# Block 0 of a latent-attention kernel: other staging places for weights, own tiles per position, latents in three loads, the rotary stack in two halves

## The chip, the core and the metric

The kernel runs on one core of one Trainium2 chip. The time is the device time of one execution in microseconds (us). Before the change three runs took 1594.83, 1597.79 and 1601.57 us; the median, 1597.79, is the figure to compare with. A further execution, recorded by the hardware profiler, took 1599.18 us; everything called "the profile" below comes from that one.

Engines go by these names: PE is TensorE (matrix products; "PEld" is its loading of stationary operands), DVE is VectorE, ACT is ScalarE, POOL is GpSimd, and SP is SyncE, which here only issues DMA. Each engine works through a queue of its own in order; ACT and POOL issue DMAs too. An instruction that has to wait holds up whatever stands behind it in its engine's queue.

## The reference

One layer with multi-head latent attention (16 heads, 2048 tokens, hidden size 512), then a linear layer, each with a residual and a layer norm:

```python
# x: [1, 2048, 512]; H=16, DN=128, DR=64, DV=128, query latent 384, key/value latent 128
cq = rms_norm(x @ w_qa.T, q_a_ln_w)                      # query latents [2048, 384]
q = (cq @ w_qb.T).reshape(b, s, H, DN + DR)              # per head: 128 plain + 64 rotary columns
q_pe = q_pe * cos + rotate_half(q_pe) * sin
ckv = x @ w_kva.T                                        # [2048, 128 + 64]
k_pe = rotary(ckv[..., 128:])                            # one rotary key for all heads
kv = rms_norm(ckv[..., :128], kv_a_ln_w) @ w_kvb.T       # per head: k_nope 128, v 128
scores = q_full @ k_full.T * (DN + DR) ** -0.5           # causal, float32 softmax
out = softmax(scores) @ v                                # [2048, 16 * 128]
x = layernorm(x + out @ w_o.T)
x = layernorm(x + x @ (weight * scale_weight[:, None]).T + bias)
```

## The kernel before

**Arithmetic.** Matrix products in single precision are made of three products of split operands: `split` (L61 to L68) writes the high part with ACT (L64, or L67 with a scale) and the rest with DVE (L65, L68). The projection of keys and values is never made per head. Instead the plain part of `w_qb` is multiplied with the key part of `w_kvb` (`weights_q`, L131 to L171), so that queries meet the 128-wide latent keys directly, and the values are the latents too. `Kn` and `Kp` (each 128 x 2 x 2048) hold all keys, the latent and the rotary part, transposed, in a high and a low plane.

**Tiling.** Queries go in four blocks of 512 rows (`b` = 0 to 3), heads in eight pairs (`p`), and a block in four positions (`qt`) of 128 rows. Block `b`, position `qt` sees `nk = (4b + qt + 1) * 128` keys. A score tile is called `s_b_p_qt` below, its values `o_b_p_qt`. `units` (L615 to L679) runs over pairs and positions. In block 0 one position of a pair is: scores of both heads in one PSUM tile (`pair_scores`, L496; its products L410), row maxima on DVE (L504), exponentials on ACT into `pr` (L510), then `pair_probs` (L518): the normalised probabilities in two half-precision parts `hl` (ACT L522, DVE L523), and one transposing DMA on SP (L524) from `hl` into `PT`. `values` (L529) multiplies `PT` with the latents in `V` (PE L540), ACT copies the result to `ot` (L545), and a DMA takes it to DRAM. `PT` is a stretch of a ring of three slots in SBUF, `ring0`, that `room` gives out; values run behind the scores by a lag in positions (L616: 2 in block 0, at most 3 later).

**Block 0 prepares everything else.** Only the first 512 rows are projected ahead. While block 0's attention runs, two side generators are advanced by the position loop (L658 to L662): `rest_of_x` makes keys, values and query latents for the other 1536 rows in half blocks `hb` = 2 to 7 (`project_x`, L187 to L265: `xr` loads on ACT's queue, keys, three tiles `ps_cq`, their squares `sq` and `acc` at L251 and L253), and `rest_of_w` makes the weights of head groups 2 and 3 (`weights_q`; group 1 is made before the loop). `query_norms` sums `acc` over partitions with PE (L272) for the norm of the query latents. Latents and weights go out to DRAM buffers `cq_d`, `wq_d`, `wpe_d` and come back when a block or a group needs them: `load_block` (L299), `load_wq` (L311), `load_wpe`. In block 0 these loads are issued by POOL, later by SP.

**Buffers.** Raw pieces of input (`xr`, and in `weights_q` `rpe` and `wqb`) share four buffers, tag `wraw`; ACT issues their loads. Split pieces on their way to DRAM (`wpst` L146, `wst` L161, `cqst` L245) share the tag `st` with two buffers of 128 x 2 x 512 words. `pr` and `hl` have two buffers each, from the pool `blk0` (L120), for all positions. PSUM in block 0 has four tiles "m" (projections, weights, values) and two score tiles "s".

**Rotary queries.** `project_pe` (L324 to L366) works on a group of four heads: two products per group, `prod` on DVE (L341), the two sums (L348, L349; POOL except for group 0), `ph` on ACT (L351), and the stack: for each head two copies (ACT in block 0 and for the first group of block 1, L360; POOL otherwise, L362) and two subtractions (DVE in those cases, except that for group 0 heads 1 and 3 are POOL's; POOL otherwise; L363) into `pe`. All four heads are one step. `project_nope` (L369 to L391) makes the plain queries `qn` of one pair and, after its second head, issues the next weight load; for the last pair of a block also the loads of the next block's latents, `cq`, 1.5 MB as one DMA, and of its cosines, `cs`.

**Order.** In block 0 the queues of all engines are laid out by a scheduler ahead of time (`schedule_with_timeline_sim=True`, L971): the written order gives priorities, and an instruction is taken when its operands and its buffers are free in the scheduler's model. So a buffer that comes free earlier can move an instruction forward in its queue. From block 1 on the order of PE and SP is the written one (`manual_schedule`, L783). `fillers` is a list of generators, `fill` (L551) advances the first one by a step; in block 0 it is called once after each position's scores and probabilities, and the projections of the next pair are what it holds.

Of the kernel before, what the change touches and what calls it, by code (L numbers as in the profile page):

```python
# [9 lines left out]
F16 = mybir.dt.float16  # L10
BF16 = mybir.dt.bfloat16
F32 = mybir.dt.float32
# [7 lines left out]
P = 128  # L20
# [3 lines left out]
LT = 3  # L24
# [25 lines left out]
def mla_block(ctx: ExitStack, tc: tile.TileContext, a, out):  # L50
# [7 lines left out]
    def move(queue, dst, src):  # L58
        queue.dma_start(dst.bitcast(F32), src.bitcast(F32))
# [57 lines left out]
    ctx_a = ctx.enter_context(ExitStack())  # L117
    psum["m"] = ctx_a.enter_context(tc.tile_pool(name="ps_m0", bufs=4, space=PSUM, side="right"))
    psum["s"] = ctx_a.enter_context(tc.tile_pool(name="ps_s0", bufs=2, space=PSUM))
    blk0 = ctx_a.enter_context(tc.tile_pool(name="blk0", bufs=2))  # L120
    pa = ctx_a.enter_context(tc.tile_pool(name="pa", bufs=1))
    pa2 = ctx_a.enter_context(tc.tile_pool(name="pa2", bufs=2))

    def split_tile(raw, n, name, step):
        h = pa.tile([P, KT, n], F32R, name=f"{name}_h")
        l = pa.tile([P, KT, n], F32R, name=f"{name}_l")
        for i in range(0, KT, step):
            split(raw[:, i : i + step], h[:, i : i + step], l[:, i : i + step])
        return h, l

    def weights_q(g, direct=None):  # L131

        if direct is None:
            wk = pa.tile([P, 4, P], F32, tag="wk", name=f"wk{g}")
            nc.scalar.dma_start(wk, a["wk"][:, 4 * g : 4 * g + 4])
        else:
            wk = direct[2]
        for lt in range(LT):
            sc = qln[:, lt : lt + 1]
            if direct is None:  # L140
                raw = pa2.tile([P, 256], F32, tag="wraw", name=f"rpe{g}_{lt}", bufs=4)
                nc.scalar.dma_start(raw, a["wpe"][:, lt, g])
            else:
                raw = direct[4][:, lt]
            if direct is None:
                to = pa2.tile([P, 2, 256], F32R, tag="st", name=f"wpst{g}_{lt}")  # L146
            else:
                to = direct[1][:, :, lt]
            split(raw, to[:, 0], to[:, 1], sc)
            move(nc.sync, wpe_d[g][:, :, lt], to)  # L150
        for lt in range(LT):
            sc = qln[:, lt : lt + 1]
            if direct is None:
                raw = pa2.tile([P, 4, P], F32, tag="wraw", name=f"wqb{g}_{lt}", bufs=4)
                nc.scalar.dma_start(raw, a["wqb"][g, :, lt])
            else:
                raw = direct[3][:, lt]
            ps = psum["m"].tile([P, 512], F32, tag="m", name=f"ps_wq{g}_{lt}")
            for j in range(4):
                nc.tensor.matmul(ps[:, j * P : (j + 1) * P], raw[:, j, :], wk[:, j, :], start=True, stop=True)  # L160
            st = pa2.tile([P, 2, 512], F32R, tag="st", name=f"wst{g}_{lt}")  # L161
            if direct is None:
                split(ps, st[:, 0], st[:, 1], sc)
                move(nc.sync, wq_d[g][:, :, lt], st)
            else:
                to = direct[0][:, :, lt]
                split(ps[:, :256], to[:, 0], to[:, 1], sc)
                split(ps[:, 256:], st[:, 0, 256:], st[:, 1, 256:], sc)
                move(nc.sync, wq_d[g][:, :, lt, :256], to)
                move(nc.sync, wq_d[g][:, :, lt, 256:], st[:, :, 256:])  # L170
            yield  # L171

    def value_output(p, pool, tag):
# [13 lines left out]
    def project_x(hb, wkv, wqa, direct=None, raws=None):  # L187
# [47 lines left out]
        for lt in range(LT):  # L235
            ps = psum["m"].tile([P, 512], F32, tag="m", name=f"ps_cq{hb}_{lt}")
            n = 0
            for kt in range(KT):
                for w_, x_ in ((wqa[0], xh), (wqa[0], xl), (wqa[1], xh)):
                    nc.tensor.matmul(  # L240
                        ps[:, :256], w_[:, kt, lt * P : (lt + 1) * P], x_[:, kt, :], start=n == 0, stop=n == 11
                    )
                    n += 1
            if direct is None:
                st = pa2.tile([P, 2, 256], F32R, tag="st", name=f"cqst{hb}_{lt}")  # L245
                split(ps[:, :256], st[:, 0], st[:, 1])
                move(nc.sync, cq_d[b][:, :, lt, half], st)
            else:
                split(ps[:, :256], direct[:, 0, lt, half], direct[:, 1, lt, half])
            sq = pa2.tile([P, 256], F32, tag="sq", bufs=1, name=f"sq{hb}_{lt}") if lt else acc  # L250
            nc.scalar.activation(sq, ps[:, :256], AF.Square, scale=(LT * P) ** -0.5)  # L251
            if lt:
                nc.vector.tensor_tensor(acc, acc, sq, ALU.add)  # L253
            if lt == 1:
                pt = psum["m"].tile([P, 2, 2, P], F32, tag="m", name=f"ps_kt{hb}")
                for i, (nk, kp) in enumerate(flip):
                    nc.tensor.transpose(pt[:, 0, i, :], nk, ident)
                    nc.tensor.transpose(pt[:, 1, i, :], kp.rearrange("p a d -> p (a d)"), ident)
                cols = slice(hb * 256, (hb + 1) * 256)
                for k_, K in ((0, Kn), (1, Kp)):  # L260
                    split(pt[:, k_].rearrange("p a c -> p (a c)"), K[:, 0, cols], K[:, 1, cols])
            yield
# [36 lines left out]
    def load_block(b):  # L299
        if b == NB:  # L300
            return
        cq = prj.tile([P, 2, LT, QB], F32R, tag="cq", name=f"cq{b}")
        if b:
            move(state["queue"], cq, cq_d[b])
        cs = prj.tile([P, 2, QB], F32, tag="cs", name=f"cs{b}")
        (state["queue"] if b else nc.sync).dma_start(cs, a["csq"][b])
        state["cq"], state["cs"] = cq, cs
# [16 lines left out]
    def project_pe(b, g, direct=None):  # L324
# [30 lines left out]
        for j in range(4):  # L355
            q = slice(32 * j, 32 * j + 32)
            for x in range(2):
                to = pe[32 * x : 32 * x + 32, j, :]
                if quick:
                    nc.scalar.activation(to, rp[q, x, :], AF.Copy)  # L360
                else:
                    nc.gpsimd.tensor_copy(to, rp[q, x, :])  # L362
                (nc.gpsimd if not quick or (b, g) == (0, 0) and j % 2 else nc.vector).tensor_tensor(  # L363
                    pe[64 + 32 * x : 96 + 32 * x, j, :], rp[q, x, :], ph[q, x, :].bitcast(F32), ALU.subtract
                )
        state["pe", b, g] = pe  # L366
        yield

    def project_nope(b, p, direct=None):  # L369
        if direct is None and ("wq", b, p) not in state:  # L370
            load_wq(b, p)
        w = state.pop(("wq", b, p)) if direct is None else direct
        cq = state["cq"]
        qn = blk.tile([P, 2, 2, QB], F32R, tag="qn", name=f"qn{b}_{p}")
        for j in range(2):
            ps = psum["m"].tile([P, QB], F32, tag="m", name=f"ps_qn{b}_{p}_{j}")
            n = 0
            for lt in range(LT):
                for i, k in ((0, 0), (0, 1), (1, 0)):
                    nc.tensor.matmul(  # L380
                        ps, w[:, i, lt, j * P : (j + 1) * P], cq[:, k, lt, :], start=n == 0, stop=n == 8
                    )
                    n += 1
            split(ps, qn[:, 0, j, :], qn[:, 1, j, :], kvln)
            if j == 1:
                state["qn", b, p] = qn
                if b or p == NPAIR - 1:
                    load_wq(*((b, p + 1) if p + 1 < NPAIR else (b + 1, 0)))
                if p == NPAIR - 1:
                    load_block(b + 1)  # L390
            yield  # L391

    def project(b, p):
# [102 lines left out]
    def pair_scores(pool, b, p, qt, nk):  # L496
# [7 lines left out]
        nc.vector.tensor_reduce(neg, ps[:, :, :nk], axis=AX.X, op=ALU.max, negate=True)  # L504
        bias = small.tile([P, 2], F32, tag="bias", name="bias")
        nc.vector.tensor_scalar(bias, neg, r, None, ALU.mult)
        pr = pool.tile([P, 2, nk], F32, tag="pr", name=f"pr{b}_{p}_{qt}")
        sums = small.tile([P, 2], F32, tag="sums", name="sums")
        for j in range(2):
            nc.scalar.activation(  # L510
# [5 lines left out]
        return pr, inv  # L516

    def pair_probs(pool, b, p, qt, nk, PT, pr, inv):  # L518
        hl = pool.tile([P, 2, 2, nk], F16, tag="hl", name=f"hl{b}_{p}_{qt}")
        for j in range(2):  # L520
            iv = inv[:, j : j + 1]
            nc.scalar.activation(hl[:, j, 0, :], pr[:, j, :], AF.Copy, scale=iv)  # L522
# [90 lines left out]
                pass  # L613

    def units(pool, ring, b):  # L615
        lag = min(ring.shape[1] // (2048 * (b + 1)) - 1, 3)  # L616

        for p in range(NPAIR):
            put_in(True)
# [23 lines left out]
            for qt in range(4):  # L643
# [2 lines left out]
                    ctx_f.enter_context(tc.manual_schedule(engines={ET.PE, ET.SP, ET.DVE, ET.Activation}))  # L646
                if (b, p, qt) == (0, NPAIR - 1, 3):
                    s0, PT = -4 * nk, prj.tile([P, 4 * nk], F16, tag="ph", name="carry")
                else:
                    s0 = room(2048 * (b + 1), ring.shape[1], 4 * nk, (b, p) == (2, NPAIR - 1) and qt > 0)  # L650
                    PT = ring[:, s0 : s0 + 4 * nk]
# [110 lines left out]
                    stop=p == NPAIR - 1 and j == 1 and n == 2,  # L762
                )

    ring0 = pa.tile([P, 3 * 2048], F16, name="ring0")
    units(blk0, ring0, 0)
    for g in side:
        for _ in g:
            pass
# [205 lines left out]
```

## Time and profile before

| | |
|---|---|
| three runs, median (lowest to highest) | 1597.79 us (1594.83 to 1601.57) |
| the profiled execution | 1599.18 us |
| its span, first to last instruction | 1597.4 us |
| mean granted TensorE clock | 0.992 |
| busy share: PE, DVE, ACT, POOL | 97%, 73%, 58%, 23% |
| 0 to 265 us (block 0 and preparation): PE, DVE, ACT busy; clock; DMA share | 239.0, 190.5, 177.2 us; 0.96; 0.76 |
| 265 to 1280 us: PE busy; clock; DMA share | 1008.0 of 1015 us; 1.00; 0.82 |
| 1280 to 1597 us: PE busy; clock; DMA share | 303.7 of 317 us; 0.99; 0.47 |
| DMA traffic | 262.5 MB in 633,032 packets, 570,288 of them under 512 bytes |

How the lines are read that follow. The first part of a page gives each engine's busy time and share of the span, and its number of instructions. The second cuts the span into 40 equal slices; a digit is the busy share of a slice in tenths. A line of windows gives a stretch's bounds and length, then busy time and instruction count of PE, PEld, DVE, ACT and POOL, the granted clock of TensorE as a fraction of full speed, the busy share of the 16 DMA engines, and GB/s. A line of waits names the waiting engine, operation and source line, behind the arrow what it waited for, and then total time, number of times and the longest. A line of one instruction has its start, its duration, engine, line and operation, output and inputs with shapes, and in brackets its wait before the start and the releaser. A line on DMAs gives the issuing queue, the tile, the duration of the issuing instruction, and under it the time from issue to landing.

### The profile page before, as it was taken

Reading aid. Unit: us, or ns where it says so; the run is one execution under the profiler, and the core shown is the slowest. Engines: PE = TensorE matmul, PEld = TensorE weight load, DVE = VectorE, ACT = ScalarE, POOL = GpSimd, SP = SyncE. Lnnn points to the kernel's source line nnn. Section 1 sums busy time; section 2 is a strip of 40 time slices with the busy share of each in tenths; the row PEclk is TensorE's granted clock in tenths of the full one; section 3 lists DMA queues with packets and bytes.
Section 4 is the critical chain, followed back from the end, with each engine's and each line's share of the span. In section 5 each row is a group of like instructions: output and inputs, shape, how many; then the busy total and the mean of one; then the engine's idle time right before and its main releaser. Section 6 shows DMA issues by size and latency. Waiting matters only on the chain. (4 is left out here: it accounts for less than half of the span.)

```text
span 1597.4 us, 24700 instructions
## 1 busy us (share of the span) xinstructions
PE 1550.6 (97%) x9130; PEld 1293.8 (81%) x9130; DVE 1164.0 (73%) x2099; ACT 926.1 (58%) x1631; POOL 364.6 (23%) x434
## 2 busy tenths in 40 slices
PE   8898998999999999999999999999999998999997
PEld 7777877888888788888888888888888886788886
DVE  6777777888787878787787777777777775455564
ACT  5767676666665766767765665665666665321120
POOL 2333234252206305050022400400400000022132
PEclk9999999999999999999999999999999999999999
DMA  6888667789897987888896888878678798433230
GB/s 210 255 211 223 173 187 163 163 165 184 166 208 159 180 158 165 164 160 168 154 222 137 165 146 168 157 144 168 137 144 170 155 230 190 145 112 129 92 113 33
DMA packets 633032, 262.49 MB, mean 164 GB/s; under 512 B 570288, under 2 KB 611376, under 8 KB 631888
## 3 DMA queue, kind: packets, MB, share of 16 engines
q1 hardware_dynamic: 621472, 233.62, 68.1%
q0 software_dynamic: 4672, 17.73, 3.6%
q10 hardware_dynamic: 6768, 9.57, 2.1%
q8 instruction: 72, 1.18, 0.3%
q14 instruction: 48, 0.39, 0.1%
HBM read 83.17 MB, written 35.13 MB: 74 GB/s over the span
## 5 line engine op out<-in xcount | busy, mean ns | idle before, releaser
L410 PE MATMUL s<-Kn,qn 128*128 128x512 f32 (+4 forms) x1920 | 519.5, 376 | 6.2 <-ACT pr L463 4.4
L463 ACT ACTIVATE pr<-s,bias,rq 128x1024 f32<-128x1024 f32 (+3 forms) x320 | 324.6, 1018 | 215.0 <-DVE bias L457 157.9
L540 PE MATMUL o<-ring,V 128*128 128x256 f16 x3252 | 395.5, 274 | 12.2 <-DMA ring<-hl 5.2
L487 DVE SCALAR_TENSOR_TENSOR hl<-pr,inv,hl 128x1024 f16<-128x1024 f32 (+7 forms) x320 | 359.4, 1136 | 40.0 <-ACT hl L484 35.2
L410 PEld LDWEIGHTS s<-Kn,qn 128*128 128x128 f32 x1920 | 338.6, 190 | 52.9 <-ACT pr L463 7.8
L540 PEld LDWEIGHTS <-V 128*128 128x128 f16 x3264 | 303.7, 98 | 92.5 <-issue 52.8
L410 PE MATMUL s<-Kp,pe 128*128 128x512 f32 (+4 forms) x1280 | 360.4, 362 | 0.0
L484 ACT ACTIVATE hl<-pr,inv 128x1024 f16<-128x1024 f32 (+7 forms) x320 | 294.5, 961 | 92.6 <-issue 34.4
L448 DVE TENSOR_REDUCE neg<-s 128x1 f32<-128x1024 f32 (+3 forms) x320 | 317.8, 993 | 37.3 <-PE s L410 34.2
L410 PEld LDWEIGHTS s<-Kp,pe 128*128 128x128 f32 x1280 | 233.1, 188 | 29.6
L348 POOL TENSOR_TENSOR prod<-prod 128x512 f32<-128x512 f32 x15 | 19.3, 1288 | 641.9 <-DVE prod L341 641.9
L380 PE MATMUL ps_qn<-cq,wq 128*128 128x512 f32 x576 | 147.0, 400 | 4.1 <-ACT ot L545 3.3
L757 PE MATMUL acc<-wvo,oh 128*128 128x512 f32 x448 | 144.2, 403 | 0.0
L363 POOL TENSOR_TENSOR pe<-prod,ph 32x512 fp32r<-32x512 f32 x92 | 140.4, 1526 | 11.0 <-issue 5.1
L380 PEld LDWEIGHTS ps_qn<-cq,wq 128*128 128x128 f32 x576 | 108.3, 192 | 25.9 <-ACT ot L545 3.9
L757 PEld LDWEIGHTS acc<-wvo,oh 128*128 128x128 f32 x448 | 83.6, 189 | 21.2 <-issue 3.8
L475 DVE TENSOR_SCALAR inv<-sums 128x1 f32<-128x1 f32 x128 | 27.0, 211 | 98.6 <-ACT pr L463 98.5
L757 PE MATMUL acc<-wvo,ol 128*128 128x512 f32 x224 | 88.2, 394 | 0.0
L336 PE MATMUL ps_pe<-cq,wpe 128*128 128x512 f32 x288 | 71.9, 395 | 1.5 <-DMA cq<-cq_d 1.4
L545 ACT ACTIVATE ot<-o 128x256 f32<-128x256 f32 x128 | 48.4, 379 | 40.9 <-PE o L540 37.1
L362 POOL CAST pe<-prod 32x512 fp32r<-32x512 f32 x88 | 66.8, 760 | 3.3
L64 ACT ACTIVATE oh<-o 128x1024 fp32r<-128x1024 f32 x28 | 29.7, 1061 | 65.1 <-PE acc L757 51.8
(140 smaller groups left out, 1586.1 us busy)
## 6 DMA issues: line engine op xcount, KB each, us to landing
wq<-wq_d SPq DMA_DIRECT2D x22, 768.0 KB, 5.7
o<-ot_d SPq DMA_DIRECT2D x32, 512.0 KB, 3.3
ot_d<-ot SPq DMA_DIRECT2D x97, 128.0 KB, 2.3
wpe<-wpe_d SPq DMA_DIRECT2D x10, 768.0 KB, 5.4
wq<-wq_d POOLq DMA_DIRECT2D x9, 768.0 KB, 6.4
wq_d<-wst SPq DMA_DIRECT2D x9, 512.0 KB, 4.4
cq_d<-cqst SPq DMA_DIRECT2D x18, 256.0 KB, 3.5
wo<-in_wo_dram SPq DMA_DIRECT2D x4, 1024.0 KB, 6.2
```

The lines of the kernel that those rows point to most:

```text
L336: nc.tensor.matmul(ps, w[:, i, lt, x * P : (x + 1) * P], cq[:, k, lt, :], start=n == 0, stop=n == 8)
L362: nc.gpsimd.tensor_copy(to, rp[q, x, :])
L363: (nc.gpsimd if not quick or (b, g) == (0, 0) and j % 2 else nc.vector).tensor_tensor(pe[64 + 32 * x : 96 + 32 * x, j, :], rp[q, x, :], ph ...
L380: nc.tensor.matmul(ps, w[:, i, lt, j * P : (j + 1) * P], cq[:, k, lt, :], start=n == 0, stop=n == 8)
L410: nc.tensor.matmul(ps[:, :w], lhs, K[:, i, c0 : c0 + w], start=n == 0, stop=n == 4)
L448: nc.vector.tensor_reduce(neg[:, ti : ti + 1], v, axis=AX.XY, op=ALU.max, negate=True)
L463: nc.scalar.activation(pr[:, c0 : c0 + n * w].rearrange("p (a c) -> p a c", a=n), v, AF.Exp, bias=bias, scale=r, accum_out=sums[:, ti : ti ...
L484: nc.scalar.activation(hl[:, 0, c], pr[:, c], AF.Copy, scale=inv)
L487: nc.vector.scalar_tensor_tensor(hl[:, 1, c], pr[:, c], inv, hl[:, 0, c], ALU.mult, ALU.subtract)
L540: nc.tensor.matmul(ps[:, :256], vt[:, i, k % 4, :], v[:, :, l, k, :], start=n == 0, stop=n == 3 * kts - 1)
L545: nc.scalar.activation(ot, ps[:, :256], AF.Copy)
L757: nc.tensor.matmul(acc, l[:, t, c], state["wvo"][p][:, i, j, :], start=p == 0 and j == 0 and n == 0, stop=p == NPAIR - 1 and j == 1 and n ...
```

## The change

All of it concerns block 0 and the preparation beside it, but for the order and number of the latents' loads, which also holds for the later blocks.

1. *Weights staged where late keys will lie.* `places` names the columns 1024 to 1535 and 1536 to 2047 of `Kn` and `Kp`, which are written with keys only by half blocks 4 to 7 of `rest_of_x`. The split pieces of `wq` of groups 1 to 3 (L161) and those of `wpe` of groups 2 and 3 (L146; two of three pieces, each in half of `A`) are put there before they go to DRAM. Only the pieces that are left use `st` tiles, which are now half as large and three.
2. *Own tiles for each position.* `pr`, `hl` and `PT` of block 0 have a tag for each of the four positions with one buffer each, in place of two buffers for all and the ring; the lag of the values in block 0 is written as 2, the value that it had.
3. *Query latents in three loads.* `load_block` issues one DMA for each third of `cq` (0.5 MB) in place of one, and stands ahead of `load_wq`.
4. *The rotary stack in two halves.* For block 0 and the first group of block 1, heads 0 and 1 are one step and heads 2 and 3 another, which is appended to `fillers`. The subtractions of group 0 that were POOL's are DVE's.

```diff
-    blk0 = ctx_a.enter_context(tc.tile_pool(name="blk0", bufs=2))
+    blk0 = ctx_a.enter_context(tc.tile_pool(name="blk0", bufs=1))
...
+    A, B, C, D = (K[:, :, c : c + 512] for c in (1536, 1024) for K in (Kn, Kp))
+    places = [
+        [(None, None, None), (B, C, D)],
+        [(A[:, :, :256], A[:, :, 256:], None), (B, C, A)],
+        [(A[:, :, :256], A[:, :, 256:], None), (B, A, B)],
+    ]
...
-            if direct is None:
-                to = pa2.tile([P, 2, 256], F32R, tag="st", name=f"wpst{g}_{lt}")
+            if direct is not None:
+                to = direct[1][:, :, lt]
+            elif places[g - 1][0][lt] is not None:
+                to = places[g - 1][0][lt]
             else:
-                to = direct[1][:, :, lt]
+                to = pa2.tile([P, 2, 256], F32R, tag="st", name=f"wpst{g}_{lt}", bufs=3)
...
-            st = pa2.tile([P, 2, 512], F32R, tag="st", name=f"wst{g}_{lt}")
             if direct is None:
+                st = places[g - 1][1][lt]
                 split(ps, st[:, 0], st[:, 1], sc)
...
-                st = pa2.tile([P, 2, 256], F32R, tag="st", name=f"cqst{hb}_{lt}")
+                st = pa2.tile([P, 2, 256], F32R, tag="st", name=f"cqst{hb}_{lt}", bufs=3)
...
-        if b:
-            move(state["queue"], cq, cq_d[b])
+        for lt in range(LT if b else 0):
+            move(state["queue"], cq[:, :, lt], cq_d[b][:, :, lt])
...
+        def stack(heads):
+            for j in heads:
...
+                    (nc.vector if quick else nc.gpsimd).tensor_tensor(
...
+            yield
+
         state["pe", b, g] = pe
-        yield
+        if quick:
+            fillers.append(stack((2, 3)))
+            yield from stack((0, 1))
+        else:
+            yield from stack(range(4))
...
+                if p == NPAIR - 1:
+                    load_block(b + 1)
                 if b or p == NPAIR - 1:
                     load_wq(*((b, p + 1) if p + 1 < NPAIR else (b + 1, 0)))
-                if p == NPAIR - 1:
-                    load_block(b + 1)
...
-        pr = pool.tile([P, 2, nk], F32, tag="pr", name=f"pr{b}_{p}_{qt}")
+        pr = pool.tile([P, 2, nk], F32, tag=f"pr{qt}", name=f"pr{b}_{p}_{qt}")
...
-        hl = pool.tile([P, 2, 2, nk], F16, tag="hl", name=f"hl{b}_{p}_{qt}")
+        hl = pool.tile([P, 2, 2, nk], F16, tag=f"hl{qt}", name=f"hl{b}_{p}_{qt}")
...
-        lag = min(ring.shape[1] // (2048 * (b + 1)) - 1, 3)
+        lag = min(ring.shape[1] // (2048 * (b + 1)) - 1, 3) if b else 2
...
+                elif b == 0:
+                    s0, PT = -4 * nk, pool.tile([P, 4 * nk], F16, tag=f"PT{qt}", name=f"PT{p}_{qt}")
...
-    ring0 = pa.tile([P, 3 * 2048], F16, name="ring0")
-    units(blk0, ring0, 0)
+    units(blk0, None, 0)
```

More of the change, by code (lines that the diff above doesn't have):

```diff
@@ L166, in weights_q @@
                 to = direct[0][:, :, lt]
+                st = pa2.tile([P, 2, 256], F32R, tag="st", name=f"wst{g}_{lt}", bufs=3)
                 split(ps[:, :256], to[:, 0], to[:, 1], sc)
-                split(ps[:, 256:], st[:, 0, 256:], st[:, 1, 256:], sc)
+                split(ps[:, 256:], st[:, 0], st[:, 1], sc)
                 move(nc.sync, wq_d[g][:, :, lt, :256], to)
-                move(nc.sync, wq_d[g][:, :, lt, 256:], st[:, :, 256:])
+                move(nc.sync, wq_d[g][:, :, lt, 256:], st)
             yield
@@ L354, in project_pe @@
         quick = b == 0 or (b, g) == (1, 0)
[L355 to L365, printed above, removed]
-        state["pe", b, g] = pe
-        yield
+        def stack(heads):
+            for j in heads:
+                q = slice(32 * j, 32 * j + 32)
+                for x in range(2):
+                    to = pe[32 * x : 32 * x + 32, j, :]
+                    if quick:
+                        nc.scalar.activation(to, rp[q, x, :], AF.Copy)
+                    else:
+                        nc.gpsimd.tensor_copy(to, rp[q, x, :])
+                    (nc.vector if quick else nc.gpsimd).tensor_tensor(
+                        pe[64 + 32 * x : 96 + 32 * x, j, :], rp[q, x, :], ph[q, x, :].bitcast(F32), ALU.subtract
+                    )
+            yield
+        state["pe", b, g] = pe
+        if quick:
+            fillers.append(stack((2, 3)))
+            yield from stack((0, 1))
+        else:
+            yield from stack(range(4))
     def project_nope(b, p, direct=None):
```

## The prediction

> **What bounds the kernel now.** I read the page first, then the stretches of the first 265 us, then the waits of TensorE (PE) and ScalarE (ACT) there. The page:
>
> ```profile
> span 1597.4 us, 24700 instructions
> PE 1550.6 (97%) x9130; PEld 1293.8 (81%) x9130; DVE 1164.0 (73%) x2099; ACT 926.1 (58%) x1631; POOL 364.6 (23%) x434
> ...
> PE   8898998999999999999999999999999998999997
> ```
>
> A slice is 40 us. From slice eight on TensorE is nearly always busy; only the first seven, block 0 and what is prepared beside it, have holes. The change lies there, so its worth is time in which TensorE stood still before about 263 us. Four stretches of that time (columns: window, length, busy us and instruction count of PE, PEld, DVE, ACT, POOL, granted TensorE clock, DMA share, GB/s):
>
> ```profile
> 40.00:60.00 20.00, 16.39 (x98) 14.07 (x97) 16.13 (x28) 15.18 (x33) 7.56 (x7) 0.91 0.86 271
> ...
> 80.00:100.00 20.00, 16.14 (x95) 13.43 (x94) 15.33 (x32) 15.32 (x35) 10.88 (x17) 0.91 0.87 188
> ...
> 130.00:150.00 20.00, 15.13 (x93) 12.14 (x92) 15.69 (x36) 12.91 (x36) 6.22 (x9) 1.00 0.98 255
> 150.00:160.00 10.00, 8.78 (x41) 7.26 (x42) 7.48 (x14) 9.30 (x20) 4.15 (x8) 0.66 0.69 176
> ```
>
> VectorE (DVE) and ACT have slack on average, and the DMA engines are nearly full. A hole costs twice: by itself, and by the clock. 0.91 over 20 us is 1.8 us lost, 0.66 over 10 us is 3.4 us. Who held TensorE between 20 and 265 us (total, times, longest):
>
> ```profile
> PE ps_rq L272 <- DVE acc L253: 4.3, 1, 4.3
> PE o L540 <- ACT ot L545: 3.8, 1, 3.8
> PE ps_wq L160 <- DMA wqb<-in_wqb_dram: 3.4, 2, 2.4
> PE ps_qn L380 <- ACT ot L545: 1.9, 1, 1.9
> PE s L410 <- ACT pr L510: 1.8, 2, 1.6
> ```
>
> With the smaller rows this is 20.9 us. Add the clock, 1.8 three times (40 to 60, 80 to 100, 245 to 265) and 3.4 once: **29.7 us is all that block 0 can give**. Behind ACT stand buffers:
>
> ```profile
> ACT hl L522 <- DMA ring<-hl: 11.5, 4, 5.2
> ACT wst L67 <- DMA wq_d<-wst: 8.9, 3, 4.3
> ...
> ACT wst L67 <- DMA cq_d<-cqst: 5.2, 2, 3.3
> ```
>
> ACT wants to write a tile whose last contents are still being stored or transposed, and everything in its queue waits along.
>
> **The change, part by part.**
>
> *Staging in the late keys, three half-size `st` tiles.* No arithmetic is added or taken away. ACT loses its 16.0 us of waits at `wst` (8.9 + 5.2 + 1.9, the last for a `wpe_d` store). The new places are reused late; one new wait can bite: the split of `wpe` of group 3 goes into `Kn` just after the store of `wq` of group 2 left there, four ACT steps earlier. A store landed after 3.7 to 7.6 us in the 135 to 152 us stretch, the TensorE work between is about 4 us: 0 to 3.6 us on ACT, 1 taken, covered by ACT's slack. The 4.3 us hole is this part's best case. ACT's queue there:
>
> ```profile
> 149.36 0.69 ACT L67 ACTIVATE wst<-ps_wq,qln 128x512 fp32r<-128x512 f32 x1 [2.71 <-DMA wq_d<-wst]
> ...
> 149.95 0.38 ACT L251 ACTIVATE sq<-ps_cq 128x256 f32<-128x256 f32 x1
> ```
>
> The square `sq`, which `acc` and then the norm's matmul wait for, stood behind the held `wst`. In the changed order of ACT it also moves up, ahead of pair 3's exponentials. The stretch from 141 to 158 us cost 1.6 (a PSUM tile not yet read by DVE) + 4.3 + clock 3.4 = 9.3 us. Bounds 0 and 9.3; I take 8.5.
>
> *Own tiles for each position.* The 11.5 us at `hl` go: each position's tile was last read a whole pair earlier. The longest is at 242.78 us, where ACT stood 5.23 us. PT per position drops the SP queue's waits for ring space; their readers are two positions behind, at no cost or gain.
>
> *The rotary stack in two halves.* For group 0, POOL's four subtractions go to DVE. In the trace the shared case is visible: DVE's four take 0.683 to 1.69 us each, together 5.74 us, while POOL's four run at 1.6 us. Eight alone on DVE are 8 x 0.683 = 5.5 us: even; but heads 0 and 1 are ready after four, 2.7 us. POOL issues the `wpe` load of group 1 some 3 us earlier, no longer behind its subtractions. In the changed queues the later stacks are emitted nearly unbroken all the same: 0.
>
> *Latents in three loads, ahead of `wq`.* On POOL two more issues at 0.56 us, 1.1 us, ahead of `wq` and the `ot` stores; nobody on the path waits for those stores. For blocks 2 and 3 two more issues on SP at 0.6 us each time, 2.4 us in all, ahead of transposes whose readers come 8 us later; uncovered they would cost those 2.4 us, and I take 0. `wq` comes 1.5 MB later, and is needed some 20 us after its issue. For block 1 TensorE waited 1.4 us for the latents (one load of 9.7 us from issue to landing).
>
> *The order that follows.* Block 0's queues are made by the scheduler, and freed tiles let it pull work forward. Two pulls matter.
>
> First, near 57 us. The splits of `wpe` of group 2 now stand in ACT's queue ahead of the first exponentials (before, after them). Their loads:
>
> ```profile
> L142 ACTq DMA_DIRECT2D rpe<-in_wpe_dram x3: 334/335/647, 52.1 to 54.0; - x3
> ...
> DMA to landing us min/median/max: 6.9/7.0/7.3
> ```
>
> Following ACT's queue with its own durations, the loads are issued at about 54 us, after `xh` of the third half block. Here the **Trainium skill** (DMA: Bandwidth & Descriptors, two cost components) would give about 2.0 us plus bytes over 436 GB/s: an estimate of 2.3 us for 128 KB, landing at 56.5, as ACT gets there, and the pull is free. The row says 7. One of the two big transfers beside them has gone earlier, so I take 4.5 us: landing at 58.5 to 59, both splits done at 60, and the exponentials about 3.3 us later than their 56.95. TensorE reaches the third score tile at 57.2; the score pool has two tiles, so it waits for the first exponential, at 61.2: 4.0 us. The pulled-up scores of the next pair then wait for the third position's exponential, while 4.4 us of other work that had filled this place comes after. Net of the 1.1 us that TensorE waited here for a transpose, 4.5 us, and 1.7 for the clock: **6.2 us lost** (1 to 8).
>
> Second, at the block's end. TensorE now takes the latents' first two parts and the values of pair 6's third position ahead of pair 7's later scores. The transposes there:
>
> ```profile
> L524 SPq DMA_TRANSPOSE ring<-hl x7: 1190/1432/6529, 225.8 to 251.8; - x7
> ...
> DMA to landing us min/median/max: 2.5/3.7/10.3
> ```
>
> The one of 10.3 us is just this position's: issued at 232.4 behind 2.3 MB of latents and weights, landed at 242.7. The bytes are the same after the change. So TensorE would stand from about 236.7 to 242.7, with scores that could have run placed behind. Against that go the old holes, 1.6 + 1.4 + 3.8 and 1.8 of clock, the 3.8 because ACT no longer loses 5.23 us. Bounds: 5 lost, 8.6 gained; I take 0, nearer to the transpose's row.
>
> *The rest.* At 40 to 46 us (3.4) the load of the third `wqb` piece leaves at about 39.5 us as before, behind the same splits: gain 0.3. From 78 to 100 us, 1.0 + 1.0 + 1.9 and 1.8 of clock hang on ACT and DVE arriving late, after 2.9 us for an `xr` load that now leaves some 15 us earlier: I take all 5.7 (bounds 0 and 5.7).
>
> **Sum:** 0.3 - 6.2 + 5.7 + 8.5 + 0 = 8.3 us gained. The profiled execution took 1599.18 us, span 1597.4 and 1.8 around it; less 8.3 it is 1590.9. The three runs have a median of 1597.79, 1.4 below: **1589.5 us**.
>
> The second rule to weigh is the skill's clock gate (TensorE: Matmul & The Clock Gate, practical table): no idle gaps over about 3 us, one idle window halves the clock. By it the 94 us hole, 1.9 us at most, would cost no clock. The row says 0.91 there: clustered short holes did it. By the rule alone the gain at 78 to 100 us is 3.9 and the sum 6.5; I keep the row. For the new 4 us stall both say that the clock falls.
>
> **The rivals.** *The pulls are free* (0.15): loads and the transpose land sooner, because the bursts are spread out. Then the 6.2 is 0 and the block's end gives 5: 0.3 + 5.7 + 8.5 + 5 = 19.5, 1578 us. For it: ACT's 35 us of DMA waits fall away. Against: DMA shares of 0.86 to 0.98.
>
> *It moves only* (0.16): the 5.7 at 78 to 100 is not won, since exponentials that are 4 us late keep the two score tiles late: 2.6 gained, 1595 us.
>
> *Slower* (0.24): ACT's queue with loads ahead of exponentials is the new bound. Place: the splits of `wpe` of groups 2 and 3, at 57 and about 120 us. Price: 8 at the first if the loads take the row's 7 us; at the second 3.6, and 1.7 for the clock; the 5.7 not won, the 8.5 halved since `sq` shares that queue: 0.3 - 8 - 5.3 + 4.2 = 8.8 us lost, 1606.6 us. It decides once the loads are over 6 us and DVE's lag passes from pair to pair; below 5 us the forecast stands.
>
> **How the numbers follow.** 0.5% of 1597.8 is 8 us, about what a measurement tells from no change: 1589.8 and 1605.8 are the bounds. The forecast has 0.45, its own range 1579 to 1597, with 0.30 of it below 1589.8 and 0.15 within. With the first rival, faster is 0.45. The second gives same 0.31. Of the slower rival all but a little lies above 1605.8: 0.24. The range goes from the free pulls with the whole of the block's end (8.6 in place of 5, near 1574) to just over the slower rival, 1608.
>
> **What would show it.** Right: no `hl` and no `wst` rows with a DMA releaser among ACT's waits; a TensorE hole of about 4 us near 58 us behind an exponential; none at `ps_rq`; clock 1.00 at 150 to 160 us; a stall on `o` near 240 us; blocks 1 to 3 of the same length within 1 us. Wrong: no hole near 58 us (first rival), holes over 2 us between 70 and 130 us (the slower one), or latents that make block 1 start late.

## The result, and the profile after

| | median of five runs | lowest to highest |
|---|---|---|
| before | 1598.22 us | 1594.83 to 1601.96 |
| after | 1607.89 us | 1607.08 to 1608.20 |

The ratio is 1.0055, with a 95% interval of 1.0036 to 1.0075: the changed kernel is slower by 9.7 us, where 8.3 us of gain were forecast. The profiled execution of the changed kernel took 1607.2 us, its span 1605.4. Its page, and seven of its stretches (columns as in the windows of the kernel before):

```profile
span 1605.4 us, 24676 instructions
PE 1549.8 (97%) x9130; PEld 1292.0 (80%) x9130; DVE 1163.5 (72%) x2103; ACT 924.8 (58%) x1631; POOL 358.1 (22%) x432
...
PE   8899987999999999999999999999999998999997
```

```profile
40.00:60.00 20.00, 15.52 (x89) 13.82 (x90) 16.32 (x34) 14.89 (x34) 3.21 (x8) 0.83 0.90 291
80.00:100.00 20.00, 19.01 (x134) 16.52 (x134) 17.42 (x35) 15.80 (x38) 10.17 (x17) 1.00 0.68 197
130.00:150.00 20.00, 16.63 (x99) 13.93 (x99) 13.71 (x30) 12.52 (x30) 5.77 (x9) 0.91 1.09 247
150.00:160.00 10.00, 9.77 (x68) 8.48 (x66) 8.23 (x20) 7.45 (x23) 5.67 (x10) 1.00 0.51 163
220.00:240.00 20.00, 12.93 (x70) 9.66 (x69) 6.85 (x17) 8.32 (x23) 6.21 (x11) 0.83 0.96 224
240.00:260.00 20.00, 14.88 (x82) 11.03 (x80) 13.37 (x23) 12.47 (x26) 5.56 (x7) 0.92 0.37 106
260.00:280.00 20.00, 13.59 (x72) 11.97 (x72) 12.20 (x28) 7.23 (x14) 2.98 (x4) 0.73 0.40 78
```

In the page's slices a hole has come at 201 to 281 us (8 and 7 in place of 9 and 8). The windows say the same: 80 to 100 and 150 to 160 us have healed, with the clock at 1.00, while from 220 to 280 us TensorE is busy for 41.4 of 60 us at a clock of 0.73 to 0.92. From 40 to 60 and from 130 to 150 us the clock is lower than before. Who held TensorE from 20 to 275 us:

```profile
PE o L559 <- DMA PT<-hl: 23.0, 5, 7.6
PE ps_wq L170 <- DMA wqb<-in_wqb_dram: 4.3, 1, 4.3
PE s L429 <- ACT pr L529: 1.6, 2, 1.3
```

The largest waits of before, 4.3 us on `acc` and 3.8 on `ot`, are gone. Five waits of values for a transposed tile have come, 23.0 us, three of them (18.6 us) after 230 us.

Where the two executions part is seen when the same products are matched in the two queues of TensorE. The queues have different orders, so only those points can be compared up to which both have finished exactly the same products; the table has such points alone. The time at which the last of them ended, after less before:

| done up to | before | after | difference |
|---|---|---|---|
| rotary queries of group 0 | 38.29 | 37.20 | -1.1 |
| weights of group 1 | 46.20 | 46.27 | +0.1 |
| s_0_0_3 | 63.18 | 62.94 | -0.2 |
| rotary queries of group 1 | 78.76 | 79.98 | +1.2 |
| o_0_1_2 | 109.50 | 106.27 | -3.2 |
| first half of the rotary queries of group 2 | 133.20 | 130.15 | -3.1 |
| first third of the query latents of half block 5 | 159.77 | 151.93 | -7.8 |
| s_0_6_3 | 231.79 | 225.08 | -6.7 |
| o_0_7_2 | 259.99 | 268.51 | +8.5 |
| o_1_3_0 | 377.61 | 385.41 | +7.8 |
| product ff9 of the linear layer | 1541.23 | 1549.08 | +7.9 |

The changed kernel was 6.7 us ahead when pair 6 ended, lost 15.2 us in the last 43 us of block 0, and carried the rest to its end. Between these two points TensorE's waits are 18.6 us, where they were 6.8. Blocks 1 to 3 are as long as before.

**What happens there.** In TensorE's queue, before: s_0_7_1, s_0_7_2, the first half of the rotary queries of block 1, o_0_6_2, the second half, s_0_7_3. After: two thirds of the first half of the rotary queries, o_0_6_2, two thirds of the second half, and only then s_0_7_1 and s_0_7_2. TensorE's timeline (start, duration, engine, operation; in brackets the wait before it):

```profile
226.77 0.40 PE L429 MATMUL s<-Kp,pe 128*128 128x256 f32 x2
227.01 1.58 PE L347 MATMUL ps_pe<-cq,wpe 128*128 128x512 f32 x6
235.67 2.10 PE L559 MATMUL o<-PT,V 128*128 128x256 f16 x9 [7.07 <-DMA PT<-hl]
237.42 2.78 PE L347 MATMUL ps_pe<-cq,wpe 128*128 128x512 f32 x6
240.04 0.39 PE L429 MATMUL s<-Kn,qn 128*128 128x256 f32 x2
...
257.34 1.46 PE L559 MATMUL o<-PT,V 128*128 128x256 f16 x6 [3.92 <-DMA PT<-hl]
266.41 2.10 PE L559 MATMUL o<-PT,V 128*128 128x256 f16 x9 [7.61 <-DMA PT<-hl]
```

And the transpose that the line at 235.67 waits for, which is the only one in 223 to 230 us:

```profile
L543 SPq DMA_TRANSPOSE PT<-hl x1: 5757/5757/5757, 223.5 to 223.5; - x1
...
DMA to landing us min/median/max: 12.2/12.2/12.2
```

It was issued at 223.5, among four loads for block 1 that POOL issued from 221.1 to 224.2 us, and landed 12.2 us later. It had taken 10.3 us before as well; there some 6 us of work (two scores of 1.7 and 2.2 us and half of the rotary queries, 2.3) and two waits of 1.6 and 1.4 us stood ahead of its reader, and TensorE came to it at 242.76, just when it had landed (242.7). The delayed scores then reach VectorE:

```profile
242.25 1.29 DVE L352 TENSOR_TENSOR prod<-ps_pe,cs 128x512 f32<-128x512 f32 x2 [10.46 <-PE ps_pe L347]
...
253.33 5.57 DVE L376 TENSOR_TENSOR pe<-prod,ph 32x512 fp32r<-32x512 f32 x8 [0.38 <-ACT ph L362]
258.93 1.22 DVE L523 TENSOR_REDUCE neg<-s 128x2 f32<-128x1024 f32 x1
...
261.51 1.14 DVE L542 SCALAR_TENSOR_TENSOR hl<-pr,inv,hl 128x384 f16<-128x384 f32 x2
```

DVE stood 10.46 us, and ACT 8.0 us for its result. When DVE gets to the eight subtractions of the rotary stack they take 5.57 us, and two things wait behind them: the maxima of s_0_7_3, whose scores were ready at 253.4, and the last part of `hl` for pair 7's third position, which DVE begins at 261.51. The transpose of that `hl` is issued at 262.7 and lands 3.6 us later; o_0_7_2 waits 7.6 us for it. Before, both stood ahead of the stack:

```profile
248.94 2.82 DVE L523 SCALAR_TENSOR_TENSOR hl<-pr,inv,hl 128x384 f16<-128x384 f32 x2
251.68 1.21 DVE L504 TENSOR_REDUCE neg<-s 128x2 f32<-128x1024 f32 x1
...
253.75 5.57 DVE L363 TENSOR_TENSOR pe<-prod,ph 32x512 fp32r<-32x512 f32 x8 [0.59 <-ACT ph L351]
```

So the first hole of 7.1 us brings two more, 3.9 and 7.6, and from 257 to 270.6 us the granted clock is 0.50.

### The profile page after: what moved, and what is told of

Its sections match the earlier page's. It is cut to its first block, busy times and chain, and to the rows that moved or that the text cites. A ratio compares the mean times of both kernels' runs of the same rounds, so it can differ in the third digit from the quotient of the medians.

```text
span 1605.4 us, 24676 instructions
## 1 busy us (share of the span) xinstructions
PE 1549.8 (97%) x9130; PEld 1292.0 (80%) x9130; DVE 1163.5 (72%) x2103; ACT 924.8 (58%) x1631; POOL 358.1 (22%) x432
## 5 line engine op out<-in xcount | busy, mean ns | idle before, releaser
L559 PE MATMUL o<-ring,V 128*128 128x256 f16 x3024 | 364.5, 274 | 5.2 <-DMA ring<-hl 3.9
L376 POOL TENSOR_TENSOR pe<-prod,ph 32x512 fp32r<-32x512 f32 x88 | 133.8, 1520 | 5.7
```

Source lines behind the costliest of these rows:

```text
L376: (nc.vector if quick else nc.gpsimd).tensor_tensor(pe[64 + 32 * x : 96 + 32 * x, j, :], rp[q, x, :], ph[q, x, :].bitcast(F32), ALU.subtract)
L559: nc.tensor.matmul(ps[:, :256], vt[:, i, k % 4, :], v[:, :, l, k, :], start=n == 0, stop=n == 3 * kts - 1)
```

## The experiments

Each median, of 4 to 22 runs, is set against the kernel before on the same chip; its medians were 1598.62 us (e1 to e4), 1599.85 (e5 to e8) and 1598.99 (e9 to e11).

| run | what it is | median us | ratio to before (95%) |
|---|---|---|---|
| e1 | changed, one load of latents behind `wq` | 1593.95 | 0.9971 (0.9960 to 0.9981) |
| e2 | before, three loads ahead of `wq` | 1621.07 | 1.0144 (1.0122 to 1.0166) |
| e3 | changed, one load ahead of `wq` | 1593.44 | 0.9965 (0.9955 to 0.9975) |
| e4 | changed, block 1's loads held | 1596.87 | 0.9992 (0.9979 to 1.0005) |
| e5 | before, staging | 1594.74 | 0.9967 (0.9955 to 0.9979) |
| e6 | before, stack in halves | 1608.82 | 1.0055 (1.0041 to 1.0070) |
| e7 | staging and stack | 1591.39 | 0.9946 (0.9933 to 0.9959) |
| e8 | e1, `wpe` in `st` tiles | 1600.75 | 1.0002 (0.9990 to 1.0014) |
| e9 | e7, five raw buffers | 1591.99 | 0.9961 (0.9946 to 0.9976) |
| e10 | e9, `wpe` in `st` tiles | 1589.36 | 0.9947 (0.9931 to 0.9963) |
| e11 | e7, `wpe` in `st` tiles | 1593.18 | 0.9962 (0.9948 to 0.9977) |

**e1: the loads as they were.**

```diff
-        for lt in range(LT if b else 0):
-            move(state["queue"], cq[:, :, lt], cq_d[b][:, :, lt])
+        if b:
+            move(state["queue"], cq, cq_d[b])
...
-                if p == NPAIR - 1:
-                    load_block(b + 1)
                 if b or p == NPAIR - 1:
                     load_wq(*((b, p + 1) if p + 1 < NPAIR else (b + 1, 0)))
+                if p == NPAIR - 1:
+                    load_block(b + 1)
```

> The changed kernel with the latents' loads as they were: one DMA, issued behind the one of wq. Theory ORDER: the 14.5 us that were lost between 230 and 270 us come from TensorE's order at the block's end, where the values of pair 6's third position and the first parts of block 1's rotary queries stand ahead of pair 7's second and third scores; that order is brought by the three loads alone. Then the end costs what it cost before, the 6.7 us won by 230 us stay, and the time is 1592 to 1594 us. Rival TILES: the transpose is late and the tail exposed because own tiles and staging let more transfers start at once; then the loads do not matter and the time stays at 1605 to 1608.

1593.95 us, 13.9 less than the changed kernel (14.3 when each is set against its own runs of before). TensorE's queue at the block's end is that of the kernel before. TILES is out: own tiles and staging are all in this kernel. The transpose of pair 6's third position still took 10.4 us to land, and nobody waited for it.

**e2: three loads alone,** the same edit the other way round, on the kernel before.

> The kernel before with only the latents in three loads, ahead of wq. ORDER: TensorE gets the same order at the block's end as in the changed kernel, so the loss of about 14 us comes alone: 1609 to 1613 us. TILES: nothing else of the change is in it, so 1597 to 1599.

1621.07 us: the loss comes with the three loads alone, and is larger than expected. TensorE's queue at the block's end is that of the changed kernel, and its waits from 225 to 280 us are of the same kind, but that the second long one, 4.0 us, is put down to ACT's split of `qn`:

```profile
PE o L540 <- DMA ring<-hl: 12.1, 2, 7.5
PE o L540 <- ACT qn L67: 4.0, 1, 4.0
```

By the matched products the block's end cost 13.3 us. The rest was not in the expectation: 2.8 us before it, 3 between 490 and 550 us and 6 at block 3's start (near 890 us), where TensorE waited 4.8 us for an exponential. ACT and DVE are laid out by the scheduler in block 1, in block 2 and at block 3's start too, and this build had them in another order at block 2's start. The changed kernel has not.

**e3: one load, but ahead of `wq`.** The diff is the first half of e1's.

> The changed kernel with one load of 1.5 MB, but still ahead of wq. In its order the whole first rotary projection stands ahead of pair 7's second score, and the values of pair 6's third position behind its third score. ORDER, in the form that it is what stands behind a late operand that costs: TensorE stands from about 227 us until the load lands near 231, 4 us and 1.7 of clock, and the late transpose is covered by two scores: 1597 to 1600. If only the lead over wq mattered, not the split: 1605 to 1608. If only the split mattered: 1592 to 1594.

1593.44 us, below the 1597 expected, and in the range given to the case that only the split matters. The first half of the rotary queries stands ahead of s_0_7_1 here, and waited 1.7 us for the latents, not 4: TensorE came to it at 231.9, and the load, issued at 225.5, landed at 233.5. The values o_0_6_2 stand behind s_0_7_2; their transpose took 10.2 us and cost nothing. So it is the place of o_0_6_2, and not that of the rotary queries, that costs; with the load ahead of `wq`, it is the split that moved it. Three loads behind `wq` were not run.

**e4: block 1's loads held back.**

```diff
+        if b == 1:
+            nc.gpsimd.tensor_copy(cq[:, 0, :, :2], state["PT62"][:, :12].bitcast(F32).rearrange("p (l c) -> p l c", l=LT))
         for lt in range(LT if b else 0):
             move(state["queue"], cq[:, :, lt], cq_d[b][:, :, lt])
...
+        if (b, p) == (1, 0):
+            nc.gpsimd.tensor_copy(w[:, 0, 0, :2], state["PT62"][:, :4].bitcast(F32))
...
+                    if (p, qt) == (6, 2):
+                        state["PT62"] = PT
+                    if (p, qt) == (6, 3):
+                        load_block(1)
+                        load_wq(1, 0)
```

> The changed kernel, with the loads for block 1 (three of latents, then wq) issued only after the transpose of pair 6's third position has landed (POOL copies two words of its result into the tiles to be loaded). Theory TRAFFIC, the second half of ORDER: that transpose takes 12.1 us to land because the 2.3 MB start just ahead of it. Then it lands within 5 us of its issue, the planner's order has both scores ahead of the rotary projection, and the time is 1591 to 1597, with a hole of up to 3 us at the latents. If the transpose is late by its own size or place in SP's queue, it lands after 10 us again and the time is 1605 or more.

1596.87 us, at the upper end of what was expected. The transpose, the only one in its stretch:

```profile
L547 SPq DMA_TRANSPOSE PT<-hl x1: 1440/1440/1440, 225.3 to 225.3; - x1
...
DMA to landing us min/median/max: 3.8/3.8/3.8
```

3.8 us in place of 12.2, and its issue 1.44 us in place of 5.76: the same transpose of the same tile. The loads beside it were the cause of its delay. TensorE's order changed with this edit too (both scores stand ahead of the rotary queries again), so the time of e4 does not tell order and traffic apart. An estimate for the order of the changed kernel: TensorE came to o_0_6_2 there at 228.6, and a transpose issued at 223.5 that takes 3.8 us would land at 227.3, with no wait. The delay is only handed on: the next transpose, issued at 234.6 behind the held loads, took 9.5 us and held TensorE for 1.9.

**e5 and e6: one part alone on the kernel before,** staging with the half-size `st` tiles in e5, `stack` in halves in e6, each with the lines of the diff above.

> The kernel before with only the staging in the late keys and the half-size st tiles. Theory of the prediction: the 4.3 us hole before ps_rq and its clock go, worth 8.5, and the early end of the wpe splits costs up to 6: 1588 to 1596 us. Rival BUNCH: what ACT no longer waits for starts its stores, loads and inputs together, and a transpose behind them lands some 10 us after its issue with the values that read it standing early in TensorE's queue (135 us in the changed kernel): the hole at ps_rq gives place to one of 3 us and its clock there, so 2 to 5 us are left: 1594 to 1597.

> The kernel before with only the rotary stack in two halves and all subtractions of group 0 on DVE. The prediction: worth nothing, 1597 to 1600 us. Rival: it delays the exponentials of the first positions, 1600 to 1604.

Staging alone wins 5 us (1594.74), within both ranges, and its trace has BUNCH's hole: 2.0 us before the values near 136 us. The stack alone, costed at nothing, loses 9 us (1608.82). The first row of ACT's waits between 20 and 265 us, and lines of its timeline:

```profile
ACT wst L67 <- DMA wq_d<-wst: 9.6, 2, 5.3
```

```profile
52.81 0.67 ACT L67 ACTIVATE qn<-ps_qn,kvln 128x512 fp32r<-128x512 f32 x1
...
58.76 0.69 ACT L67 ACTIVATE wst<-ps_wq,qln 128x512 fp32r<-128x512 f32 x1 [5.29 <-DMA wq_d<-wst]
...
60.60 0.46 ACT L517 ACTIVATE pr<-s,bias,rq 128x128 f32<-128x128 f32 x1 [0.63 <-DVE bias L513]
```

The shorter stack let the scheduler move things: the third `wst` split waits 5.29 us for its tile ahead of the first exponentials, which begin at 60.6 us in place of 56.95. From 46 to 75 us this profile loses 10.7 us against the kernel before. That this wait is the cause of them is argued, not isolated. With staging that tile is free, and the two parts together (e7) are better than staging alone.

**e7: shared tiles.** e1, with `pr`, `hl` and the ring as before.

> The changed kernel with one load of latents behind wq, and with shared pr, hl and the ring as before: only staging and the stack are left of the change. If own tiles are worth what ACT waited at hl near 242 us (5.2 us, of which 3.8 were TensorE's), the time is 3 to 6 us above that of the version with one load (1594): 1597 to 1600. If ACT's waits at hl are covered: 1593 to 1595.

1591.39 us, below all that was expected. ACT's waits at `hl` are back:

```profile
ACT hl L541 <- DMA ring<-hl: 11.5, 6, 5.2
```

They are 11.5 us, as before the change, and cost nothing that shows. Against its own runs of before e7 is 3.8 us better than e1. By the profiles 1.6 of it lie in blocks 2 and 3, half of that at block 3's start, where DVE has another order; the rest is less than what two executions of one queue differ by (below). So own tiles won nothing; whether they cost something stays open.

**e8 and e11: `wpe` of groups 2 and 3 in `st` tiles,** with own tiles and with shared ones.

```diff
-        [(A[:, :, :256], A[:, :, 256:], None), (B, C, A)],
-        [(A[:, :, :256], A[:, :, 256:], None), (B, A, B)],
+        [(None, None, None), (B, C, A)],
+        [(None, None, None), (B, A, B)],
```

> The changed kernel with one load of latents behind wq, but wpe of groups 2 and 3 split into the three st tiles, so that their splits stand behind the first exponentials again and their stores wait for tiles. By the prediction's step at 57 us (6.2 lost to those splits) it is 5 to 7 us better than the version with one load: 1587 to 1589. By the changed kernel's profile, in which the loads landed 3.1 us after their issue and ACT waited 1.2 us only, that step is worth 1.5 at most; by BUNCH the later stores also take away the hole of 3.3 us and 3.4 of clock near 135 us: 1588 to 1592. If the stores that wait hold up ACT as they did before: 1595 to 1599.

> The version with one load, wpe in st, and shared tiles. With own tiles it took 1600.8 us, of which some 6 us were lost only at block 3's start (near 866 us), where TensorE waited 4.8 us for an exponential; ACT's order at block 2's start had changed there too. Here ACT has the order of the kernel before at block 2's start. If that order, and nothing in block 0, was the loss, the stall is gone and the time is 1588 to 1593. If the loss comes from block 0: 1597 to 1602.

e8 took 1600.75 us, above all three of its ranges. In its profile it was 6.6 us ahead of the kernel before at the end of block 0, and lost 6.3 at block 3's start:

```profile
PE s L429 <- ACT pr L482: 4.8, 1, 4.8
```

That is one wait between 860 and 880 us; ACT's order at block 2's start is the one of e2. e11, with ACT's usual order there, has 0.6 us in its place and took 1593.18 us, just above the first of its ranges. So block 0 was not what made e8 slow. Why that order ends in a wait some 350 us later was not followed.

**e9 and e10: the space of own tiles spent on a fifth raw buffer.**

```diff
-                raw = pa2.tile([P, 4, P], F32, tag="wraw", name=f"wqb{g}_{lt}", bufs=4)
+                raw = pa2.tile([P, 4, P], F32, tag="wraw", name=f"wqb{g}_{lt}", bufs=5)
```

The other two kinds of pieces with the tag `wraw` likewise.

> The version with staging and stack, shared tiles and one load of latents (1591.4 us), with five raw input buffers in place of four: the space that own tiles took is spent there. In all versions with staging TensorE waits 3.9 to 4.4 us near 44 us for the third wqb piece of group 1, whose load waits for a raw buffer, and the clock is halved for 6.8 us there. If that load now leaves earlier: 4 us and 1.7 to 3.4 of clock are won, 1584 to 1587. If its landing is late by the other inputs beside it: 1590 to 1593. If the earlier inputs delay the transposes near 65 and 134 us more: above 1593.

> The same with five raw buffers, and wpe of groups 2 and 3 in the st tiles. Near 134 us fewer transfers start together (BUNCH), so the hole of 4.0 us and 1.7 of clock there shrink: 2 to 5 us better than the version with five raw buffers and staged wpe. If the stores that wait hold up ACT: 2 to 6 us worse.

e9 took 1591.99 us: the wait for `wqb` near 44 us is gone, and one of 4.1 us for the `wq` of pair 1 stands in its place. That is the second of its ranges. e10 took 1589.36 us, 2.6 below e9, as expected, but their intervals lie over each other; the transpose that BUNCH speaks of landed 7.0 us after its issue there, and TensorE did not wait for it. e7 and e10 are the shortest of all, 0.54 and 0.53% below the kernel before, and no difference between them shows.

## Why the prediction was wrong

**The step that failed is the block's end, which was costed at 0 between 5 lost and 8.6 gained.** It lost 14.5 us by the matched products (15.2 up to o_0_7_2, of which 0.7 came back in block 1), and 13.9 by the medians of e1 and the changed kernel. The place and the cause were in the text: the pull of o_0_6_2 ahead of the scores, the transpose of 10.3 us behind 2.3 MB, "TensorE would stand from about 236.7 to 242.7, with scores that could have run placed behind". That hole was 6 us by the prediction and 7.1 in the trace. The error was to set the old holes against it as gains. By name they went, but new ones came where they had stood: the chain of pair 7 (scores, maxima, exponentials, `hl`, transpose, values) starts 7 us late with nothing left to hide it, DVE takes the rotary stack ahead of the last `hl` and the last maxima, and waits of 3.9 and 7.6 us stand in place of the 3.8 us on `ot`. So TensorE's waits grew from 6.8 to 18.6 us where they were to shrink; the other 3.4 of the 15.2 are left to the clock of 0.73 to 0.92. The lower bound, 5, is less than the hole of 6 us that the text had worked out, and leaves nothing for the clock; what waits behind the hole was not followed to the block's end. With the block's end as before (e1) the rest of the change gains 4.7 us, where 8.3 were forecast.

The other steps follow by the matched products. One execution tells little about each: e1 and e3 have the changed kernel's queues up to s_0_7_0, and where they differ from it their figures stand beside.

**Near 57 us, 6.2 lost:** 1.5 in the changed kernel's profile (from -0.2 to +1.2), but 5.3 in e1 and 6.2 in e3. The loads:

```profile
L150 ACTq DMA_DIRECT2D rpe<-in_wpe_dram x3: 334/568/767, 51.9 to 53.5; - x3
...
  DMA rpe<-in_wpe_dram: 1.2, 1
...
DMA to landing us min/median/max: 3.2/3.8/4.1
```

They landed in 3.2 to 4.1 us, between the row of before (7.0) and the 2.3 us of the Trainium skill (DMA: Bandwidth & Descriptors, Anatomy of one DMA, two cost components), a fit that the page gives for transfers issued by GpSimd, while ACT issues these. They were issued up to 2 us earlier than the walk through ACT's queue had it. ACT waited 1.2 us; the first exponential came at 57.08, 0.1 later than before, and not 3.3. TensorE's wait for an exponential, at 64 to 65 us, is 1.3 us in all three runs, not 4.0. What makes the step large in e1 and e3 is another wait, for the transpose of the first position, and the clock of 0.83 from 60 to 80 us that goes with it. In the changed kernel this wait is 1.0 us and the clock 1.00; the first two rows are e1, the third is e3:

```profile
PE o L559 <- DMA PT<-hl: 2.6, 1, 2.6
60.00:80.00 20.00, 16.12 (x95) 13.87 (x95) 12.93 (x37) 12.67 (x37) 2.57 (x6) 0.83 0.88 205
PE o L559 <- DMA PT<-hl: 4.2, 1, 4.2
```

So the order was right; the mechanism was not, and where the size came out at 6.2 (e3), that was luck.

**40 to 46 us, 0.3 gained:** 1.2 lost (from -1.1 to +0.1). The third `wqb` piece was waited for 4.3 us in place of 2.4, and the clock was halved for 6.8 us there in place of 3.4.

**78 to 100 us, 5.7 gained:** 4.5 (from +1.2 to -3.2), and 5.4 in e1 and e3. TensorE's waits fell by 2.9 us, where 3.9 were forecast. The clock went from 0.91 to 1.00, worth 1.7, so on the clock the row was the better guide than the skill's rule of 3 us (TensorE: Matmul & The Clock Gate, Why this matters for your kernels), by which holes of at most 1.9 us cost no clock.

**141 to 158 us, 8.5 gained:** the hole before `ps_rq` went and the clock is 1.00, as said, 9.3 us with the 1.6 before it, but only 4.8 net were gained (from -3.1 to -7.8), and 1.1 of them were lost again up to s_0_6_3 without a wait. A new hole stands at 133 us, 3.4 us and 1.7 of clock, which no step had; e1, e3 and e4 have it too (3.3, 2.9 and 4.6 us). Three stores of 256 KB, a load of 768 KB and two inputs of 256 KB begin between 118.1 and 119.9 us, once nothing makes ACT wait (before, transfers of these kinds were spread from 121.4 to 128.5); the transpose issued behind them at 123.2 landed 10.3 us later, and o_0_2_2 had been moved ahead of s_0_3_2. The hole comes with staging (2.0 us in e5, 4.0 in e7). With `wpe` in `st` that transpose lands after 7.0 to 7.8 us (e8, e10, e11), but in e8 and e11 a wait of 2.2 and 3.0 us on DVE stands in the same place, and in e10 one of 2.0 on an exponential: the bunching is shown, its price is not separated.

**The stack, 0:** true only together with staging. Alone it costs 9 us (e6). **Own tiles:** the 11.5 us at `hl` went as said and were worth nothing (e7). **Blocks 1 to 3 unchanged within 1 us:** they were, +7.8 and +7.9. The 1.1 us at the start, where the clock from 0 to 20 us was 1.00 in place of 0.91, are luck: e1, e3, e4 and e7 do not repeat them (0.0 to 0.4). With 0.1 gained in the stretches between, the sum is 1.1 - 1.2 - 1.5 + 4.5 + 4.8 - 1.1 + 0.1 - 14.5 = 7.8 lost. One sum of the prediction is off without harm: the waits of TensorE from 20 to 265 us add to 21.7 us, not 20.9.

Of the rivals, the slower one has the right time, 1606.6 us, by luck: its stalls at 57 and 120 us behind late loads on ACT are not in the trace. "The pulls are free" fell with the block's end, though its sign, no hole near 58 us, was there. Of the forecast's own signs the hole of 4 us near 58 was missing; "a stall on `o` near 240 us" was there, at 235.

## What to carry to other kernels

Where a scheduler lays out the queues, look for which wait stands in front of what: a late operand cost nothing as long as two scores stood ahead of its reader (e1, e3), and 14 us when the reader stood ahead of them. A hole at the end of a stage is priced by following the whole chain behind it; here 7.1 us grew to 15.2. Waits on a full buffer can also space transfers out, as near 120 us here: take them away, and ask which small transfer on the path now starts among the large ones.

## What the runs showed of the hardware

A transposing DMA of 384 KB, issued within 3 us behind loads of 2.3 MB, took 9.7 to 12.2 us from issue to landing, and its issue 5.3 to 6.6 us (before, after, e1, e2, e3); held apart from them 3.8 and 1.4 (e4).

Executions with the same queues differ by more inside block 0 than expected. The changed kernel, e1 and e3 have one order on TensorE, ACT and DVE up to s_0_7_0; at the end of s_0_6_3 their profiled executions were 6.7, 1.9 and 2.3 us ahead of the kernel before. The transpose of the first position landed 4.8 us after its issue in the first of them, 6.3 in e1 and 8.0 in e3. A gain of a few us in this stretch can only be read from many runs.

Edits to block 0 (in e2 also to the loads of the later blocks, which the changed kernel has too) changed the order of ACT and DVE in blocks 1 to 3, and at block 3's start the profiles with another order lie between 6 us lost (e2, e8: another order of ACT at block 2's start) and 1.7 won (e5, e10: another order of ACT and DVE at block 3's start), as much as some parts of the change itself.
